# One-hot in spare PSUM columns ahead of the products; nodes' gating and residual tile by tile (a graph network layer on one core)

## The chip, the cores and the metric

The kernel runs on one core of a Trainium2 chip. The time is device time in microseconds (us), the median of three runs. The core has five engines that work at once, each through its own queue in order: PE (matmuls), DVE (elementwise), ACT (activations and copies), POOL (here it issues the indirect loads) and SP (it issues plain loads and stores). SBUF is the working memory, PSUM the small memory that PE writes into. The profile is one execution recorded by the hardware profiler.

## The reference

A layer of message passing on 12,500 nodes with 160 features (64 scalars and 32 vectors of 3) and 400,000 edges, which come sorted by destination. Cut to what matters:

```python
h_s = s @ lin1_ws * a * inv(64);  h_v = einsum('nci,cd->ndi', v, lin1_wv) * a * inv(32)
w   = silu(edge_scalars @ fc_w1 * inv(64)) @ fc_w2 * inv(64)      # 224 weights per edge
es, ev = h_s[edge_src], h_v[edge_src]                             # gather, 160 numbers per edge
m_s1 = w1 * es * e0;              m_s2 = w4 * (ev . e1) * inv(3)
m_v1 = (w2 * es) x e1;  m_v2 = w3 * ev * e0;  m_v3 = w5 * cross(ev, e1) * inv(2)
agg  = segment_sum([m_s1, m_s2], [m_v1, m_v2, m_v3], edge_dst) / 4
pre  = self_connection(x) + lin2(agg)
scalars = silu(pre_s[:, :64]);  gates = sigmoid(pre_s[:, 64:96]); gated = gates * pre_v
out  = layernorm(x + concat(scalars, gated))
```

## The kernel before

A first stage of 62 us multiplies all nodes by lin1 and writes the table `h_tab` to DRAM. Then the edges go by in 3125 tiles of 128 edges, four tiles at a time: a *quad*, 782 of them (the last has one tile). Which quad a tile belongs to is fixed in `steps`; `slot_of` is its place in that order.

The order of the work on PE, DVE, ACT and POOL is written out by hand: the loop at L811 issues one step per quad, and each engine runs its instructions in the order in which they are issued there. For quad n a step issues

- `gather` (L448, L452): four indirect loads on POOL, one per tile, each of 128 rows of `h_tab`, into `hg` (four buffers of a quad each, so the gather of quad n+4 reuses the buffer of quad n);
- `weights` (L457, L465): on PE, the edges' 224 weights of each tile into `pw`, a PSUM tile of 4 x 256 columns, of which columns 224 to 255 of each tile are unused. There are two such tiles, used in turn, so quad n+2 writes where quad n was;
- `products` (L469): on DVE, one multiplication at L475 and three at L483, from `pw` (PSUM) and `hg` (SBUF) into `pr`. Between them come pieces of older work (`add_up`, the nodes' `rest`);
- `select_quad` (L523): on DVE, the one-hot `oh` at L529, which compares the edges' relative destinations `rel` with `iota`, and `sel` at L532, the one-hot times the four edge attributes `eas`. All five are in SBUF;
- the additions `add` (L571) into the nodes' sums `acc`, and one step of the nodes' work, `step_on`;
- `sum_up` of quad n-2 (L766, L539): on PE, `sel` transposed times `pr`, into `pa`;
- `hide` of quad n+2 (L443, L445), and, when due, the turning of finished blocks (L548 to L553), their second linear map (L563, L566) and the self connection (L712).

The framework adds the waits. It takes a `pw` tile as one whole here: the matmuls of quad n+2 wait for the last instruction that reads quad n's tile, and a DVE instruction that writes into the tile waits for the quad's matmuls.

Nodes whose edges are all done are finished in jobs of up to four tiles of 128 nodes (`finish`, L574): 23 jobs of four tiles, one of two, and the last of four, whose last tile is not full. A job runs as one step each for turning every tile (L597, L598), `gates` (ACT, L604), `gated` (DVE, L608 and L609, from `z` and `sg` into `y`), `residual` (DVE, L616, `y` plus the nodes' input `xt`), `moments` (L621, L623), `root` (L627) and `norm` (L631, L633, and the store at L636). `z`, `sg`, `y` and `xt` are in SBUF. The last job runs after the loop, in the tail.

Of the kernel before, what the change touches and what calls it, by code (L numbers as in the profile page):

```python
# [10 lines left out]
F32 = mybir.dt.float32  # L11
# [9 lines left out]
P = 128  # L21
S = 64
V = 32
V3 = 3 * V
# [6 lines left out]
W = 16  # L31
Q = 4
# [3 lines left out]
AHEAD = 3 * CT  # L36
# [4 lines left out]
NWT = 224  # L41
# [12 lines left out]
def gnn_kernel(  # L54
# [21 lines left out]
    nc = tc.nc  # L76
# [58 lines left out]
    slot_of = {}  # L135
# [88 lines left out]
    with tc.tile_pool(name="nodes", bufs=len(starts)) as nodes, tc.tile_pool(  # L224
        name="nodes_ps", bufs=6, space=PSUM
# [83 lines left out]
        for c0, cn, quarters, cq, xa, xz in loaded:  # L309
# [3 lines left out]
            nt = -(-cn // P)  # L313
            first = c0 // P
            full = cn // P
            for t0 in range(0, nt, U):
                ps = nps.tile([P, U, P], F32, name="hp")
                for t in range(t0, min(t0 + U, nt)):
                    n = min(P, cn - t * P)
                    nc.tensor.matmul(ps[:n, t - t0], xa[:, t * P:t * P + n], l1,  # L320
                                     start=True, stop=True)
                k = min(U, full - t0)
# [3 lines left out]
                if t0 + k < nt <= t0 + U:  # L326
                    n = cn - full * P
# [6 lines left out]
            for u in range(-(-cq // P)):  # L334
                n = min(P, cq - u * P)
# [10 lines left out]
            if cn > full * P:  # L346
                n = cn - full * P
# [35 lines left out]
    for to, part, pieces, w, r0, c0, by in maps:  # L383
        for k, piece in enumerate(pieces):
# [3 lines left out]
            m = terms.setdefault((to, part, four), len(terms))  # L388
# [131 lines left out]
            sorted_eat[a0] = eas  # L520
        return sorted_eat[a0]

    def select_quad(pool, tiles):  # L523

        n = len(tiles)
        t0 = slot_of[tiles[0][0]]
        u = t0 % AHEAD
        oh = pool.tile([P, Q, W], F32, name="oh4")[:, :n]
        nc.vector.tensor_tensor(oh, rel[:, t0:t0 + n, None].to_broadcast([P, n, W]),  # L529
                                iota[:, None, :].to_broadcast([P, n, W]), op=OP.is_equal)  # L530
        sel = pool.tile([P, Q, 4, W], F32, name="sel", bufs=3)
        nc.vector.tensor_mul(  # L532
            sel[:, :n], oh[:, :, None, :].to_broadcast([P, n, 4, W]),
            by_slot(tiles[0][0])[:, u:u + n, :, None].to_broadcast([P, n, 4, W]))
        return sel
# [38 lines left out]
    def finish(fin, psum, t0, nt, p, most=NF):  # L574


        whole = nt if p == P else nt - 1
        xt = fin.tile([P, most, D], F32, name="xt", bufs=2)
        held = []
        if whole < nt:  # L580
            nc.vector.memset(xt[:, whole], 0.0)
        parts = [(slice(t0 * P, (t0 + whole) * P), slice(0, whole), P)] if whole else []
        if whole < nt:
            parts.append((slice((t0 + whole) * P, (t0 + whole) * P + p), slice(whole, nt), p))
        for nodes_of, k, n in parts:
            nc.sync.dma_start(xt[:n, k], x[nodes_of, :].rearrange("(t p) d -> p t d", p=n))

        def turn(k):
            if not held:
                held.extend(fin.tile([P, most, *shape], F32, name=name) for name, shape in (  # L590
                    ("z", [2 * V3]), ("sg", [V3]), ("y", [D]), ("st", [6]), ("mv", [2]),
                    ("rs", [])))
            z = held[0]
            c = (t0 + k) * P
            pp = psum.tile([P, 2, V3], F32, name="pp", tag="misc")
            for m in range(2):
                nc.tensor.transpose(pp[:, m], acc[:, m, c:c + P], ident[:V3, :V3])  # L597
            return lambda: nc.vector.tensor_scalar(  # L598
                z[:, k], pp.rearrange("p m c -> p (m c)"), at[:, t0 + k:t0 + k + 1], None,
                op0=OP.mult)  # L600

        def gates():
            z, sg = held[:2]
            nc.scalar.activation(sg[:, :nt], z[:, :nt, :V3], AF.Sigmoid)  # L604

        def gated():
            z, sg, y = held[:3]
            nc.vector.tensor_mul(y[:, :nt, :S], z[:, :nt, :S], sg[:, :nt, :S])  # L608
            nc.vector.tensor_mul(  # L609
                y[:, :nt, S:].rearrange("p t (c i) -> p t i c", i=3),  # L610
                z[:, :nt, V3:].rearrange("p t (i c) -> p t i c", i=3),
                sg[:, :nt, None, S:].to_broadcast([P, nt, 3, V]))

        def residual():
            y = held[2]
            nc.vector.tensor_add(y[:, :nt], y[:, :nt], xt[:, :nt])  # L616

        def moments():
            _, _, y, st, mv, _ = held
            for k in range(nt):  # L620
                nc.vector.bn_stats(st[:, k], y[:, k])  # L621
            for k in range(nt):
                nc.vector.bn_aggr(mv[:, k], st[:, k])  # L623

        def root():
            mv, rs = held[4:]
            nc.scalar.activation(rs[:, :nt], mv[:, :nt, 1], AF.Sqrt, bias=eps)  # L627

        def norm():
            _, _, y, _, mv, rs = held  # L630
            nc.vector.reciprocal(rs[:, :nt], rs[:, :nt])  # L631
            for k in range(nt):
                nc.vector.tensor_scalar(y[:, k], y[:, k], mv[:, k, 0:1], rs[:, k:k + 1],  # L633
                                        op0=OP.subtract, op1=OP.mult)
            for nodes_of, k, n in parts:
                nc.sync.dma_start(out[nodes_of, :].rearrange("(t p) d -> p t d", p=n), y[:n, k])  # L636

        return [lambda k=k: turn(k) for k in range(nt)] + [
            gates, gated, residual, moments, root, norm]


    tiles_of_nodes = -(-N // P)
# [5 lines left out]
    with tc.tile_pool(  # L648
        name="fin", bufs=1
# [132 lines left out]
        def add_up(n):  # L782

            if not adds or adds[0][0] > n:
                return []
            _, b, os, k, base = adds.pop(0)
            waiting.discard(blocks_of(b // 2)[b % 2])
            return [(base, os, k)]
# [15 lines left out]
        with tc.manual_schedule(engines={ENG.PE, ENG.DVE, ENG.Activation, ENG.Pool}):  # L804
            fetch(0)
            hide(0)
            waits = []
            pieces = list(range(0, N, CHN))
            products_due = []
            checks = farthest(late)  # L810
            for n, (c, i, tiles) in enumerate(steps):  # L811
                if 2 <= n < 2 + ZP // 2:
                    for k in range(2):
                        clear(2 * (n - 2) + k)
                if n in checks:
                    checks[n]()
                fetch(n + 4)
                hg = gather(deep, [index(t) for t, _, _ in tiles])
                pw = weights(pw_ps, hids[c, i // 2], [(half, u - i // 2 * 4) for _, half, u in tiles])

                rest = turning.pop(0)() if turning else None
                step_on = not rest and doing.pop(0) if doing and not turning and not rest else None
                ready = []

                def first(n=n):
                    if rest:
                        rest()
                    ready.extend(add_up(n))

                pr = products(edge, pw, hg, len(tiles), [first, lambda n=n: ready.extend(add_up(n))])  # L830
                sel = select_quad(edge, tiles)
                for a in ready:
                    add(*a)
                if step_on:
                    step_on()
                begin()
                waits.append((tiles, pr, sel))
                if len(waits) > 2:
                    sum_up(n, *waits.pop(0))
                hide(n + 2)  # L840
                for blocks, in due(maps_due, n):
                    output(n, blocks)
                for j, sa in due(turns_due, n):
                    turn_blocks(n, j, sa)
                if products_due:
                    products_due.pop(0)()()
                if n % 30 == 13 and pieces:
                    products_due.extend([lambda: (lambda: None)] * 3 + self_connection(pieces.pop(0)))
            assert not pieces and not products_due
            last_steps = finish(fin, misc_ps, *last_job, most=LAST)  # L850
            n = len(steps)
            while waits:
                sum_up(n, *waits.pop(0))
            while turns_due or maps_due:
                n += 1
                for blocks, in due(maps_due, n):
                    output(n, blocks)
                for j, sa in due(turns_due, n):
                    turn_blocks(n, j, sa)
            assert len(adds) <= NO  # L860
            n += 2
            while adds:
                for a in add_up(n) + add_up(n):
                    add(*a)
            while turning or doing or to_do:
                begin()
                for f in turning:
                    f()()
                for f in doing:
                    f()  # L870
                turning.clear()
                doing.clear()
            for f in last_steps[:LAST]:
                f()()
            for f in last_steps[LAST:]:
                f()
# [113 lines left out]
```

## Time and profile before

| | |
|---|---|
| median of three runs | 4050.34 us (4040.81, 4050.34, 4052.72) |
| the profiled execution: its time, its span | 4037.76 us, 4036.0 us |
| granted TensorE clock, mean | 0.965 |
| first gather starts, last gather ends | 61.74 us, 4003.11 us |
| busy, first stage (0 to 62 us) | PE 37.64, DVE 29.36, ACT 3.46, POOL 14.52 us |
| busy, one stretch of the loop (2000 to 3000 us) | PE 916.83, DVE 605.60, ACT 230.25, POOL 758.95 us |
| busy, tail (4003 to 4036 us) | PE 16.70, DVE 14.43, ACT 8.94, POOL 0.11 us |

An engine's busy time counts its instructions, not what its queue spends between them. A row of the groups of instructions reads: line, engine, operation, output<-inputs with their shapes, count | busy us, mean ns of one | idle us of that engine just before them, and who ended most of it. The loop is even: its three stretches of a thousand microseconds (1000 to 4003) differ by less than 1% in the busy time of PE, DVE and POOL.

### The profile page before, as it was taken

To read this page: it belongs to the slowest core of one execution; us is meant where nothing else is said; L and a number is where in the kernel's file an instruction comes from. 1 tells how busy PE (TensorE), PEld (TensorE's weight loads), DVE (VectorE), ACT (ScalarE), POOL (GpSimd) and SP (SyncE) were. 2 spreads that over 40 slices of the span, in tenths; PEclk is the share of its full clock that TensorE was granted. 3 is DMA by queue.
4 is the path that set the end of the run, shared out by engine and by line. 5 is a ranking of instruction groups with operands and counts; after the bars stand their busy time and mean duration, and the time that the engine had idled before them with its cause. 6 is when DMAs were issued, how large, how long until landed. Compare 5 with 4: busy or idle time off the path is not lost. (4 is left out here: it accounts for less than half of the span.)

```text
span 4036.0 us, 46681 instructions
## 1 busy us (share of the span) xinstructions
PE 3679.1 (91%) x14291; PEld 1590.5 (39%) x14291; DVE 2436.6 (60%) x6386; ACT 939.4 (23%) x2463; POOL 3003.9 (74%) x3144
## 2 busy tenths in 40 slices
PE   6999899999989999989998999899898999999997
PEld 4344343333334433333333334334343333333443
DVE  5656655665655655656656656556665665655665
ACT  2222121221222222212212222122122221222222
POOL 4777777777777777777777777777777777777775
PEclk8999999999999999999999999999999999999999
DMA  8344443444444434444444444444444443444442
GB/s 242 94 99 96 98 105 94 104 103 94 104 96 100 107 93 101 105 96 101 106 94 100 95 104 102 94 105 98 98 105 95 105 101 94 103 101 97 98 97 57
DMA packets 227691, 411.71 MB, mean 102 GB/s; under 512 B 71883, under 2 KB 157383, under 8 KB 226535
## 3 DMA queue, kind: packets, MB, share of 16 engines
q0 software_dynamic: 152272, 266.53, 27.6%
q1 hardware_dynamic: 74646, 142.01, 14.7%
q8 instruction: 115, 1.88, 0.2%
q14 instruction: 144, 1.18, 0.1%
q10 hardware_dynamic: 514, 0.10, 0.0%
HBM read 392.41 MB, written 16.00 MB: 101 GB/s over the span
## 5 line engine op out<-in xcount | busy, mean ns | idle before, releaser
L452 POOL DMA_INDIRECT hg<-h_tab,idx x3125 | 2989.7, 957 | 958.5 <-issue 866.6
L465 PE MATMUL pw<-w,hid 128*128 128x448 f32 x3126 | 1376.1, 564 | 194.4 <-DVE pr L483 165.7
L475 DVE TENSOR_TENSOR pr<-pw,hg 128x512 f32<-128x512 f32 x782 | 539.8, 690 | 1460.8 <-DMA hg<-h_tab,idx 967.6
L539 PE MATMUL pa<-pr,sel 128*64 128x416 f32 x6250 | 1307.9, 540 | 0.0
L483 DVE TENSOR_TENSOR pr<-pw,hg 128x384 f32<-128x384 f32 x2346 | 1153.8, 547 | 0.0
L465 PEld LDWEIGHTS pw<-w,hid 128*128 128x128 f32 x3126 | 555.6, 194 | 680.7 <-issue 442.2
L539 PEld LDWEIGHTS pa<-pr,sel 128*64 128x64 f32 x6250 | 389.6, 140 | 820.2 <-issue 680.8
L732 ACT COPY sa<-pa 128x416 f32<-128x416 f32 x521 | 263.7, 506 | 1450.4 <-PE pa L539 1447.9
L443 PE MATMUL misc<-es,w 128*128 128x512 f32 (+1 forms) x784 | 449.4, 656 | 15.6 <-DMA es<-in_es_t_dram 13.8
L445 ACT ACTIVATE hid<-misc 128x512 f32<-128x512 f32 x392 | 233.6, 596 | 739.3 <-PE misc L443 738.8
L548 PEld LDWEIGHTS misc<-ident,sa 128*128 128x128 f32 x2084 | 240.0, 141 | 310.3 <-issue 250.9
L532 DVE TENSOR_TENSOR sel<-oh,eas 128x256 f32<-128x256 f32 x782 | 338.3, 433 | 38.6 <-DVE oh L529 0.9
L563 PE MATMUL misc<-tt,l 128*96 128x256 f32 (+5 forms) x1496 | 346.1, 379 | 3.5 <-DVE z L598 2.0
L548 PE MATMUL misc<-ident,sa 128*128 128x128 f32 x2084 | 327.5, 280 | 0.8 <-DVE acc L713 0.7
L551 ACT COPY tt<-misc 128x192 f32<-128x192 f32 x521 | 164.8, 316 | 513.1 <-PE misc L548 510.6
L563 PEld LDWEIGHTS misc<-tt,l 128*96 128x96 f32 (+1 forms) x1496 | 227.0, 162 | 141.6 <-issue 73.0
L443 PEld LDWEIGHTS misc<-es,w 128*128 128x128 f32 x784 | 119.3, 192 | 283.1 <-issue 228.2
L571 DVE TENSOR_TENSOR acc<-acc,os 96x32 f32 x1042 | 193.5, 186 | 25.9 <-ACT os L566 6.9
L529 DVE TENSOR_TENSOR oh<-rel,iota 128x64 f32<-128x64 int16 x782 | 170.5, 218 | 0.0
L597 PE MATMUL misc<-ident,acc 96*128 96x96 f32 x196 | 36.8, 274 | 103.8 <-DVE acc L571 83.6
L553 ACT COPY tt<-misc 128x64 f32<-128x64 f32 x521 | 116.6, 224 | 0.0
L566 ACT COPY os<-misc 96x512 f32<-96x512 f32 (+2 forms) x68 | 38.3, 564 | 303.3 <-PE misc L563 282.7
(84 smaller groups left out, 633.3 us busy)
## 6 DMA issues: line engine op xcount, KB each, us to landing
es<-in_es_t_dram SPq DMA_DIRECT2D x258, 384.0 KB
hg<-h_tab,idx POOLq DMA_INDIRECT x3125
h_tab<-ht POOLq DMA_DIRECT2D x6, 1280.0 KB
xt<-in_x_dram SPq DMA_DIRECT2D x23, 320.0 KB
out_dram<-y SPq DMA_DIRECT2D x23, 320.0 KB
xv<-in_xv_t_dram SPq DMA_DIRECT2D x25, 187.5 KB
xs<-in_xs_t_dram SPq DMA_DIRECT2D x25, 125.0 KB
xa<-in_xs_t_dram SPq DMA_DIRECT2D x6, 512.0 KB
```

The costliest lines, as they stand in the source:

```text
L443: nc.tensor.matmul(ph[:k, c], w1[:k, :k], es[:k, t0 * P + c0 * P:t0 * P + c1 * P], start=True, stop=True)
L445: nc.scalar.activation(hid[:k, c], ph[:k, c], AF.Silu, scale=1.0 / math.sqrt(64))
L452: nc.gpsimd.indirect_dma_start(out=hg[:, t, :], out_offset=None, in_=h_tab, in_offset=bass.IndirectOffsetOnAxis(ap=i, axis=0))
L465: nc.tensor.matmul(pw[:, t:t + m, :NWT], hid[:m * S, c * P:(c + 1) * P], w2[:m * S, :m], start=True, stop=True)
L475: nc.vector.tensor_mul(two, pw[:, :n, :2 * S].rearrange("p t (k c) -> p t k c", k=2), hg[:, :n, None, :S].to_broadcast([P, n, 2, S]))
L483: nc.vector.tensor_mul(pr[:, :n, first:first + V3].rearrange("p t (i c) -> p t i c", i=3), pw[:, :n, None, 2 * S + k * V:2 * S + (k + 1) * ...
L532: nc.vector.tensor_mul(sel[:, :n], oh[:, :, None, :].to_broadcast([P, n, 4, W]), by_slot(tiles[0][0])[:, u:u + n, :, None].to_broadcast([P ...
L539: nc.tensor.matmul(pa[half * ROWS:(half + 1) * ROWS, :NPR], sel[:, t].rearrange("p k w -> p (k w)"), pr, start=start, stop=stop)
L548: nc.tensor.transpose(pt[:, four * P:four * P + k], sa[:k, c:c + P], ident[:k, :k])
L563: nc.tensor.matmul(po[:, k, :nb], l2[r, terms[to, part, four]], a[:, :nb], start=(n == 0), stop=(n == len(of) - 1))
L571: nc.vector.tensor_add(window, window, os[:, :, b])
L732: nc.scalar.copy(sa, pas.pop(j)[:, :NPR])
```

## The change

The one-hot moves from a buffer in SBUF into columns 224 to 239 of each tile of the quad's `pw`, and its instruction moves ahead of the four products; the selection reads it there and stays behind the products. In `finish`, all jobs but the last do the gating and the residual with one instruction per tile of 128 nodes in place of one for all tiles of the job.

```diff
-    def select_quad(pool, tiles):
+    def one_hot(tiles, pw):
 
         n = len(tiles)
         t0 = slot_of[tiles[0][0]]
-        u = t0 % AHEAD
-        oh = pool.tile([P, Q, W], F32, name="oh4")[:, :n]
+        oh = pw[:, :n, NWT:NWT + W]
         nc.vector.tensor_tensor(oh, rel[:, t0:t0 + n, None].to_broadcast([P, n, W]),
                                 iota[:, None, :].to_broadcast([P, n, W]), op=OP.is_equal)
+        return oh
+
+    def select_quad(pool, tiles, oh):
+
+        n = len(tiles)
+        u = slot_of[tiles[0][0]] % AHEAD
         sel = pool.tile([P, Q, 4, W], F32, name="sel", bufs=3)
         nc.vector.tensor_mul(
             sel[:, :n], oh[:, :, None, :].to_broadcast([P, n, 4, W]),
...
         whole = nt if p == P else nt - 1
+        spans = [(0, nt)] if t0 + nt == tiles_of_nodes else [(k, k + 1) for k in range(nt)]
...
         def gated():
             z, sg, y = held[:3]
-            nc.vector.tensor_mul(y[:, :nt, :S], z[:, :nt, :S], sg[:, :nt, :S])
-            nc.vector.tensor_mul(
-                y[:, :nt, S:].rearrange("p t (c i) -> p t i c", i=3),
-                z[:, :nt, V3:].rearrange("p t (i c) -> p t i c", i=3),
-                sg[:, :nt, None, S:].to_broadcast([P, nt, 3, V]))
+            for k, m in spans:
+                nc.vector.tensor_mul(y[:, k:m, :S], z[:, k:m, :S], sg[:, k:m, :S])
+                nc.vector.tensor_mul(
+                    y[:, k:m, S:].rearrange("p t (c i) -> p t i c", i=3),
+                    z[:, k:m, V3:].rearrange("p t (i c) -> p t i c", i=3),
+                    sg[:, k:m, None, S:].to_broadcast([P, m - k, 3, V]))
 
         def residual():
             y = held[2]
-            nc.vector.tensor_add(y[:, :nt], y[:, :nt], xt[:, :nt])
+            for k, m in spans:
+                nc.vector.tensor_add(y[:, k:m], y[:, k:m], xt[:, k:m])
...
+                oh = one_hot(tiles, pw)
                 pr = products(edge, pw, hg, len(tiles), [first, lambda n=n: ready.extend(add_up(n))])
-                sel = select_quad(edge, tiles)
+                sel = select_quad(edge, tiles, oh)
```

## The prediction

> **What bounds the kernel now.** I read the page's busy shares first, then its groups of instructions (busy us, mean ns | idle us before them and who ended it):
>
> ```profile
> PE 3679.1 (91%) x14291; PEld 1590.5 (39%) x14291; DVE 2436.6 (60%) x6386; ACT 939.4 (23%) x2463; POOL 3003.9 (74%) x3144
> ...
> L452 POOL DMA_INDIRECT hg<-h_tab,idx x3125 | 2989.7, 957 | 958.5 <-issue 866.6
> L465 PE MATMUL pw<-w,hid 128*128 128x448 f32 x3126 | 1376.1, 564 | 194.4 <-DVE pr L483 165.7
> ...
> L483 DVE TENSOR_TENSOR pr<-pw,hg 128x384 f32<-128x384 f32 x2346 | 1153.8, 547 | 0.0
> ...
> L532 DVE TENSOR_TENSOR sel<-oh,eas 128x256 f32<-128x256 f32 x782 | 338.3, 433 | 38.6 <-DVE oh L529 0.9
> ...
> L529 DVE TENSOR_TENSOR oh<-rel,iota 128x64 f32<-128x64 int16 x782 | 170.5, 218 | 0.0
> ```
>
> PE's 91% draws the eye, but the gathers on POOL (L452) decide. Their 2989.7 us busy and 958.5 us before them make 3948.2 us. The first starts at 61.74 us, after 6.87 us of that idle time, so the row fills the span from 54.87 to 4003.1 us without a hole. The view of the line's own instructions gives min/median/max:
>
> ```profile
> L452 POOL DMA_INDIRECT hg<-h_tab,idx x3125: 942/946/1670, 61.7 to 4002.2; - x196
> ```
>
> Over the trace's gathers I counted the pause before each next one: 303 to 313 ns, always, so POOL never waits for a buffer, PE or DVE. 2903 of 3125 gathers last 942 to 955 ns, 945.6 on average. The span is therefore 61.7 us of start + 3125 x (946 + 305 ns) = 3909 us + what single gathers last longer + 33 us behind the last one. That third term is 2989.7 - 3125 x 0.946 = 33.4 us, and it is all that this change can win on POOL. The timeline shows what makes it (start, us, engine, line):
>
> ```profile
> 712.23 0.42 DVE L608 TENSOR_TENSOR y<-z,sg 128x256 f32<-128x256 f32 x1
> 712.38 1.61 POOL L452 DMA_INDIRECT hg<-h_tab,idx  x1 [0.30 <-DMA hg<-h_tab,idx]
> ...
> 712.57 0.67 DVE L609 TENSOR_TENSOR y<-z,sg 128x384 f32<-128x384 f32 x1
> ...
> 716.77 0.81 DVE L616 TENSOR_TENSOR y<-y,xt 128x640 f32<-128x640 f32 x1
> 716.80 1.61 POOL L452 DMA_INDIRECT hg<-h_tab,idx  x1 [0.30 <-issue]
> ...
> 1181.67 0.42 DVE L532 TENSOR_TENSOR sel<-oh,eas 128x256 f32<-128x256 f32 x1
> 1181.72 1.20 POOL L452 DMA_INDIRECT hg<-h_tab,idx  x1 [0.30 <-issue]
> ...
> 2001.90 1.48 DVE L483 TENSOR_TENSOR pr<-pw,hg 128x384 f32<-128x384 f32 x3
> ...
> 2002.19 0.95 POOL L452 DMA_INDIRECT hg<-h_tab,idx  x1 [0.30 <-issue]
> ```
>
> The selection of 1181.67 ends at 2.09, and the gather that began at 1.72 lasts 1.20 us, not 0.95. The residual of 716.77 costs its gather 0.66 us; the gating pair of 712.23 and 712.57 costs 0.66 us, held through both. Three products (2001.90) lie over a gather that keeps its 0.95. The difference: selection, gating and residual have both inputs in SBUF, a product reads pw from PSUM. Laid against all gathers, the rule of the rows is sharp. A DVE instruction with two SBUF inputs that starts at least 40 ns before the gather and ends over 127 ns after the gather's start (192 for L609) lengthens it by exactly the excess; one that starts later costs it almost nothing. By the instruction whose end fits, the 33.4 us are: sel L532 151 gathers, 23.5 us; L616 9, 4.4; L609 12, 4.0; L608 3, 0.4; oh L529 25, 1.2; others, at the start above all, about 1, less rounding. Products: 3128 instructions, one gather, 0.02 us.
>
> A check on size: with starts spread evenly over a period of 1251 ns, an instruction of length d costs (d - 167)²/(2 x 1251) ns. For sel (425 ns at the median) that is 26.6 ns x 782 = 20.8 us (23.5 counted), for oh (216) 0.8 us (1.2 counted), for the three node instructions 298 ns x 24 = 7.2 us (8.8 counted).
>
> **The change part by part.** (1) *sel reads its one-hot from PSUM.* It then has the products' form, one input in PSUM and one in SBUF. Bounds: 23.5 us won (the product rows) to 0 (if the SBUF input alone were what blocks; the 2346 L483 rows, with one SBUF input each, speak against it). I take 23.5. Its own length: the product rows give 690 ns for 512 and 547 for 384, so 0.40 us for 256 against 0.43 now; nothing changes.
>
> The Trainium skill, "SBUF — State Buffer", section "Who interferes with whom", has a sentence that speaks against all this: a two-input tensor_tensor was seen not to stall DMAs, since descriptor generation needs the write interface and it takes only the read one (marked there as inferred). By that sentence part 1 would be worth 0; the rows of 716.80 and 1181.72 above say that here it does stall, so the rows stand.
>
> (2) *oh is written to PSUM, ahead of the products.* rel and iota stay in SBUF, so it keeps blocking. No row shows DVE writing PSUM; the nearest are 164 ns (16 elements) and 218 (64) into SBUF and 291 (a 128-element product out of PSUM), and I take 218. What can change is its place in the gather's period, now the end of pw's matmuls or of DVE's work before it: computed from the old trace, 20 to 37 of 782 such points fall into the 50 ns that block, at shifts of up to 150 ns. I take 1.2 us as now, 0 net; bounds +1.2 (never) and 782 x 51 ns = 40 lost (always at the worst point). On DVE it is a 0.22 us move, plus about 0.04 us of gap between oh and its reader, which now falls before the products. In 61% of quads DVE idles at least 0.26 us there (page: 1460.8 us in all), which hides it; elsewhere the products end 0.26 us later and sel no later than now.
>
> (3) *The wait that moves.* A pw bank pair is now free for quad n+2's matmuls when sel n has read it, not when the third product has: 0.43 + 0.04 us later. Queued on PE behind L465 are the sums L539 of quad n, which need that sel anyway. Today the wait shows as
>
> ```profile
> PE pw L465 <- DVE pr L483: 165.7, 78, 5.5
> ```
>
> so 78 of 782 quads feel it; 78 x 0.47 = 37 us more PE idle. What is late next is products n+2, then the freeing of hg, then the gather of quad n+6. From the third product of n to the first gather of n+4 the trace has 10.9 us at the median, 7.6 at the 5th percentile, 3.4 at least after the first five quads (0.6 at 82.7 us, once). 0.5 us is lost in that: 0, bound 1 us at the start. Uncovered, it is the third rival.
>
> (4) *Gating and residual tile by tile* in 23 jobs of four tiles and one of two (the last job is unchanged): 2 + 1 instructions become 8 + 4. The rows by shape:
>
> ```profile
> L616 DVE TENSOR_TENSOR y<-y,xt 128x640 f32<-128x640 f32 x24 | 19.6, 817 | 0.0
> ...
> L609 DVE TENSOR_TENSOR y<-z,sg 128x384 f32<-128x384 f32 x24 | 16.3, 678 | 0.0
> L608 DVE TENSOR_TENSOR y<-z,sg 128x256 f32<-128x256 f32 x24 | 10.0, 417 | 0.6 <-ACT sg L604 0.6
> ...
> L616 DVE TENSOR_TENSOR y<-y,xt 128x320 f32<-128x320 f32 x1 | 0.5, 479 | 0.0
> ...
> L609 DVE TENSOR_TENSOR y<-z,sg 128x192 f32<-128x192 f32 x1 | 0.4, 406 | 0.0
> ...
> L608 DVE TENSOR_TENSOR y<-z,sg 128x128 f32<-128x128 f32 x1 | 0.3, 282 | 0.0
> ```
>
> The last three are the two-tile job, so each length has two points: fixed 141 to 147 ns (L609 135) plus 1.056 ns per element (L609 1.41). One tile costs 214 (L608), 271 (L609), 310 ns (L616); a job 4 x 795 = 3.18 us against 1.91, so 23 x 1.27 + 0.4 = 30 us more on DVE, inside its 1599 us of idle time, since no gather or sum of that step waits for y. For the gathers the formula gives 4 x (0.9 + 4.3 + 8.2) = 53 ns a job, 1.3 us in all. But 1 of the 4 gathers that L608 held was held on through L609 without a gap. With a quarter held on, 0.94 held gathers a job x 1/3 x 0.25 us adds 0.08 us a job, 1.9 in all. So 3.3 us stay of 8.8: 5.5 won. Bounds: 8.8 won, and a loss: were each train of pieces held as one block (1.94 and 1.24 us), 1.7 us a job, 40 us in all, 31 more than now.
>
> (5) No DMA moves: SP's and POOL's queues keep their orders, out's transfer is issued from the same step. In the tail (33 us) the last job keeps its long instructions; the last full quad waits for its gather (1.84 us idle), so oh is hidden there: 0 to 0.3 us won, taken as 0.
>
> Sum: 23.5 + 5.5 = 29.0 us. The profiled execution took 4037.8 us for its span of 4036.0; it becomes 4007.0 and 4008.8. It lies 12.6 us below the median of 4050.3, under all three timed runs. I know no row for that offset, so I take 29.0 from the mean of all four executions, 4045.4: **4016**.
>
> **Rivals.** *A: sel blocks from PSUM as well* and only part 4 works: 4045.4 - 5.5 = 4040. For: half its input still comes from SBUF, and the edit doesn't take oh's own two SBUF inputs away. Against: the L483 rows. *B: the pieces hold like one train:* 4045.4 - 23.5 + 31 = 4053. For: 712.38; against: three of four freed at L608's end. *C, the slower one: the later release of pw makes PE the pace.* PE needs 3679.1/782 = 4.70 us a quad, POOL afterwards 4 x 1.252 = 5.01, so 0.30 us is spare. If all quads felt the 0.47 us, each would cost 0.17 us more, 133 us in all: 4149. It decides from 0.30/0.47, 64% of the quads, on; today 10% wait there, and PE has 357 us of idle time already. Half of this price is still slower by over 1%.
>
> **How the numbers follow.** Forecast 0.82, A 0.07, B 0.04, C 0.05, an unseen gain or loss of a few us around the bound 0.02. A measurement here tells 0.3% (12 us) from no change; 4038 is the border. Forecast and little else falls under it: faster 0.84, same (A, B) 0.10, slower (C) 0.06. Range: below, the floor of POOL 61.7 + 3909 + 33 = 4004, about all 33 us won and no offset; above, half of sel's gain with the offset, 4050.3 - 12 = 4038.
>
> **What would show it.** The gather row near 2961 us (mean 947 or 948, not 957), pause still 305 ns; sel over gathers of 0.95 us; oh with about its 1.2 us; L465's wait now on sel, longer than 165.7 us, without a gap in POOL. I am wrong if gathers of 1.1 to 1.2 us still end with sel, if pauses over 0.31 us appear on POOL (C), or if trains of small gating pieces end gathers of over 1.3 us (B).

## The result and the profile after

The changed kernel takes 4018.96 us, the median of six runs (4017.94 to 4022.50); before takes 4043.76 us over six runs, the three shown and three more. The ratio is 0.9935, 95% interval 0.9922 to 0.9948: 25 us, 0.65%, shorter.

The page of the changed kernel (busy shares, then groups of instructions; lines behind `select_quad` have moved: oh is L528, sel L537, the sums L544):

```profile
PE 3676.3 (92%) x14291; PEld 1588.0 (40%) x14291; DVE 2410.5 (60%) x6596; ACT 938.7 (23%) x2463; POOL 2982.9 (74%) x3144
...
L452 POOL DMA_INDIRECT hg<-h_tab,idx x3125 | 2968.7, 950 | 962.2 <-issue 865.5
L465 PE MATMUL pw<-w,hid 128*128 128x448 f32 x3126 | 1376.5, 564 | 191.5 <-DVE sel L537 150.1
...
L528 DVE TENSOR_TENSOR pw<-rel,iota 128x64 f32<-128x64 int16 x782 | 178.4, 228 | 468.3 <-PE pw L465 465.5
...
L537 DVE TENSOR_TENSOR sel<-pw,eas 128x256 f32<-128x256 f32 x782 | 323.6, 414 | 0.0
```

Gathers last 2968.7 us in all, not 2989.7, and the mean is 950 ns, not 957. The pauses between them are 303 to 315 ns, all 3124, as before: POOL still paces and still waits for nobody. The span fell by 19.0 us, from 4036.0 to 4017.0: 21.0 us shorter gathers, a first gather that starts 3.7 us later (65.42 against 61.74 us) and a tail 1.7 us shorter.

The timeline around one selection (start, us, engine, line):

```profile
2438.48 0.41 DVE L537 TENSOR_TENSOR sel<-pw,eas 128x256 f32<-128x256 f32 x1
...
2438.55 0.95 POOL L452 DMA_INDIRECT hg<-h_tab,idx  x1 [0.30 <-issue]
```

This sel starts 67 ns before the gather and ends 0.35 us after the gather's start. By the prediction's rule that position would have cost 0.22 us; now the gather has its 0.95. Over the whole trace 254 sels stand where they would have held a gather, and these gathers last 945.5 ns on average, none over 960. The next lines are the nodes' residual in four pieces:

```profile
3605.81 1.02 DVE L624 TENSOR_TENSOR y<-y,xt 128x160 f32<-128x160 f32 x4
...
3606.19 1.59 POOL L452 DMA_INDIRECT hg<-h_tab,idx  x1 [0.30 <-issue]
...
3606.75 0.22 DVE L528 TENSOR_TENSOR pw<-rel,iota 128x64 f32<-128x64 int16 x1
```

The gather at 3606.19 is held through the pieces and on through the one-hot that follows them at 3606.75: 1.59 us, as long as the gather under the single long residual (1.61 us at 716.80 before).

The excess of the gathers over 946 ns, by the instruction whose end fits, in us (a count over each trace; "to oh's end" are gathers held by node pieces and let go at the end of a one-hot directly behind; "oh alone" are all others let go at its end, also those that began under an addition or a sel ahead of it. Their sum is firm, the split between these two columns only to about 1 us):

| kernel | gathers in all | sel | nodes | nodes, to oh's end | oh alone |
|---|---|---|---|---|---|
| before | 2989.7 | 23.5 | 8.8 | 0 | 1.2 |
| changed | 2968.7 | 0 | 3.4 | 6.8 | 2.5 |
| e1 one-hot's part alone | 2965.0 | 0 | 3.9 | 2.1 | 2.5 |
| e2 tile by tile alone | 3006.0 | 33.8 | 8.0 | 0 | 1.2 |
| e3 one-hot ahead, in SBUF | 2995.1 | 19.1 | 0.3 | 15.2 | 4.0 |
| e4 one-hot in PSUM, behind | 2967.1 | 0 | 8.7 | 0 | 1.2 |
| e5 iota in PSUM too | 2963.3 | 0 | 8.1 | 0 | 0 |
| e6, e10 one piece a step | 2966.7, 2960.3 | 0 | 3.3, 3.5 | 0 | 0 |

The runs e1 to e4 were on a chip like that of the result, but e5 to e12 were on three chips where the granted TensorE clock was 0.87 to 0.89 on average and not 0.96 and before itself takes 5007 to 5067 us, so their times are compared with before on the same chip alone.

### The profile page after: what moved, and what is told of

Read it like the earlier page. It is cut to its first block, busy times and chain, and to the rows that moved or that the text cites. A ratio compares the mean times of both kernels' runs of the same rounds, so it can differ in the third digit from the quotient of the medians.

```text
span 4017.0 us, 46675 instructions
## 1 busy us (share of the span) xinstructions
PE 3676.3 (92%) x14291; PEld 1588.0 (40%) x14291; DVE 2410.5 (60%) x6596; ACT 938.7 (23%) x2463; POOL 2982.9 (74%) x3144
## 5 line engine op out<-in xcount | busy, mean ns | idle before, releaser
L452 POOL DMA_INDIRECT hg<-h_tab,idx x3125 | 2968.7, 950 | 962.2 <-issue 865.5
L465 PE MATMUL pw<-w,hid 128*128 128x448 f32 x3126 | 1376.5, 564 | 191.5 <-DVE sel L537 150.1
L544 PE MATMUL pa<-pr,sel 128*64 128x416 f32 x6250 | 1303.5, 539 | 0.0
L544 PEld LDWEIGHTS pa<-pr,sel 128*64 128x64 f32 x6250 | 388.0, 139 | 812.3 <-issue 799.4
L528 DVE TENSOR_TENSOR pw<-rel,iota 128x64 f32<-128x64 int16 x782 | 178.4, 228 | 468.3 <-PE pw L465 465.5
L537 DVE TENSOR_TENSOR sel<-pw,eas 128x256 f32<-128x256 f32 x782 | 323.6, 414 | 0.0
```

The costliest lines, as they stand in the source:

```text
L452: nc.gpsimd.indirect_dma_start(out=hg[:, t, :], out_offset=None, in_=h_tab, in_offset=bass.IndirectOffsetOnAxis(ap=i, axis=0))
L465: nc.tensor.matmul(pw[:, t:t + m, :NWT], hid[:m * S, c * P:(c + 1) * P], w2[:m * S, :m], start=True, stop=True)
L537: nc.vector.tensor_mul(sel[:, :n], oh[:, :, None, :].to_broadcast([P, n, 4, W]), by_slot(tiles[0][0])[:, u:u + n, :, None].to_broadcast([P ...
L544: nc.tensor.matmul(pa[half * ROWS:(half + 1) * ROWS, :NPR], sel[:, t].rearrange("p k w -> p (k w)"), pr, start=start, stop=stop)
```

## The experiments

The theories, by the letters that the expectations use: L, the forecast's, gathers are held by DVE instructions with two SBUF inputs and POOL paces; O, the new order gains; T, the short node pieces gain; W, time on DVE and the wait for pw decide; later R, the time for which pw is occupied.

**e1, the one-hot's part alone.**

```diff
-        spans = [(0, nt)] if t0 + nt == tiles_of_nodes else [(k, k + 1) for k in range(nt)]
+        spans = [(0, nt)]
```

> The one-hot's part alone; gating and residual stay one instruction per job. Theory L (a DVE instruction with two SBUF inputs over a gather's start holds the gather, and POOL paces): sel's 23.5 us are gone as in the changed kernel, the node instructions cost about 9 to 11 us again; the gathers last 2965 to 2972 us in all, time 4015 to 4023, the changed kernel's within 0.1%. Rival T (the short node pieces carry a good part of the gain): at least 5 us longer than the changed kernel, gathers 2974 us or more.

4020.61 us (4014.16 to 4022.87), ratio to before 0.9937 [0.9924, 0.9951]; gathers 2965.0 us. The changed kernel's ratio is 0.9935: as far as the intervals tell (5 us), the whole gain is the one-hot's.

**e2, tile by tile alone:** before's `select_quad`, the changed `finish`.

> Gating and residual tile by tile alone; the one-hot stays in SBUF behind the products. L: sel keeps its 20 to 25 us; trains of pieces hold gathers as the single long instructions did, but behind them come products and not a one-hot, so 5 to 9 us for the nodes; gathers 2985 to 2992 us in all, time 4038 to 4046, no change from before within 0.2%. Rival T: gathers 2983 us or less, time under 4036.

4046.20 us, ratio 1.0004 [0.9995, 1.0013] over 11 runs: no gain, so rival T falls twice. The profiled execution was the longest of the 11 (4056.16 us), and its gathers, 3006.0 us, lie outside what was expected: in it sel held 197 gathers and not 151, 10 us more, and undisturbed gathers took about 2 ns more, 6 us in all. So where sel happens to fall can move an execution by 10 us.

**e3, the changed order, the one-hot in SBUF.**

```diff
-        oh = pw[:, :n, NWT:NWT + W]
+        oh = pool.tile([P, Q, W], F32, name="oh4")[:, :n]
```

> The changed kernel with the one-hot in an SBUF buffer again, but still ahead of the products: the order is the changed one, only the memory differs. L: sel has two SBUF inputs again and costs 18 to 28 us: gathers 2987 to 2997 us, time 4038 to 4050, as slow as before. Rival O (taking the one-hot off the chain behind the gather's landing is what helped): time within 5 us of the changed kernel's 4019.

4046.11 us, ratio 1.0004 [0.9995, 1.0014]. The page of e3:

```profile
L452 POOL DMA_INDIRECT hg<-h_tab,idx x3125 | 2995.1, 958 | 960.3 <-issue 860.6
...
L537 DVE TENSOR_TENSOR sel<-oh,eas 128x256 f32<-128x256 f32 x782 | 324.8, 415 | 0.0
```

sel has the changed kernel's place and length (415 ns against 414) and only the one-hot's memory differs, yet the gathers last 2995.1 us and the gain is gone. Rival O falls; L stands. The node pieces show what they do when sel, adds, pieces and one-hot all have two SBUF inputs and follow one another: 15.2 us held to a one-hot's end.

**e4, the one-hot in PSUM but behind the products.**

```diff
-                oh = one_hot(tiles, pw)
                 pr = products(edge, pw, hg, len(tiles), [first, lambda n=n: ready.extend(add_up(n))])
+                oh = one_hot(tiles, pw)
```

> The changed kernel with the one-hot in PSUM but issued behind the products, ahead of sel. L: sel costs nothing, the one-hot alone 1 to 3 us, and trains of node pieces are no longer followed by the one-hot but by products with a PSUM input, so the 6.8 us of gathers held to the one-hot's end shrink: gathers 2962 to 2967 us in all, time 4011 to 4018, somewhat shorter than the changed kernel. pw is freed 0.23 us later than in the changed kernel; if that wait mattered (rival W), time over 4022 with pauses over 0.32 us on POOL. Rival O: time back near 4040.

4018.56 us (4015.97 to 4024.83), ratio 0.9941 [0.9928, 0.9955], gathers 2967.1 us: the changed kernel's time, not the somewhat shorter one expected. No gather is held to a one-hot's end any more, but the pieces hold 8.7 us among themselves, against 10.1 with the one-hot behind them. The one-hot lasts 236 ns there, longer than in the changed kernel, and yet holds only 1.2 us. Pauses on POOL stay at 312 ns or less: the later release of pw costs nothing here (W falls).

**e5, iota in PSUM too.**

```diff
+            for t in pw_ps.tiles:
+                nc.vector.tensor_copy(t[:, NWT + W:256], iota)
...
-                                iota[:, None, :].to_broadcast([P, n, W]), op=OP.is_equal)
+                                pw[:, 0:1, NWT + W:].to_broadcast([P, n, W]), op=OP.is_equal)
```

> The changed kernel, and iota read from the last 16 spare columns of the same PSUM tile, so that the one-hot too has one SBUF input. L: the one-hot's own 2.5 us go, and trains of node pieces end with their last piece and not with the one-hot: 10.1 us for the nodes become 5 to 8; gathers 2959 to 2965 us, time 4008 to 4015. Rival W (time on DVE and the wait for pw matter, not inputs): no change from 4019.

On a chip with clock 0.88: 5095.52 us, ratio 1.0177 [1.0137, 1.0218]. The gathers are as L expected, 2963.3 us, and no gather is held by a one-hot; the time says nothing on L, since POOL doesn't pace there (e9).

**e6, one node piece a step**, on top of e5: `finish` returns each tile's L615, L616 and L624 as a step of its own for jobs with t0 < 80.

> As the run with iota in PSUM, and for the first 20 jobs only one piece of gating or residual per step, so that a piece stands alone among products with a PSUM input; the later jobs whole, so that the tail is kept. L: 20 jobs at 53 ns a job by the formula are 1 us, the four other jobs 0.37 us each, 1.5 us: nodes 2 to 4 us in all, gathers 2956 to 2960 us, time 4005 to 4012, the shortest of all kernels here. Rival (short pieces alone hold as much as trains): like the run with iota in PSUM.

5108.26 us, ratio 1.0190 [1.0157, 1.0222]. Nodes hold 3.3 us, as expected; the gathers are 2966.7 us, outside it, since in this execution even undisturbed ones took about 2 ns more.

**e7 and e8, the price by itself:** behind each sel one more multiplication of its size, with both inputs in SBUF (e7) or one in PSUM (e8).

```diff
+        spare = pool.tile([P, Q, 4, W], F32, name="spare")
+        nc.vector.tensor_mul(spare[:, :n], X.to_broadcast([P, n, 4, W]),
+                             by_slot(tiles[0][0])[:, u:u + n, :, None].to_broadcast([P, n, 4, W]))
```

X is `iota[:, None, None, :]` in e7 and `oh[:, :, None, :]` in e8.

> The changed kernel and, behind each selection, one more multiplication of the same size with both inputs in SBUF (iota by the edge attributes) whose result nobody reads. L: (425 - 167)^2/(2 x 1251) ns x 782 = 21 us by the formula, up to 30 where node pieces and adds follow and lengthen the train: gathers 2988 to 3000 us, time 4039 to 4052. Rival W: equal to the same kernel with a PSUM input.

> The same extra multiplication with one input in PSUM (the one-hot) and one in SBUF, so the same DVE time, 0.41 us x 782 = 324 us more, and pw freed 0.41 us later still. L: costs nothing on POOL: gathers 2966 to 2972 us, time 4016 to 4024. Rival W: 20 us or more above the changed kernel.

5119.65 us, ratio 1.0222 [1.0179, 1.0264], and 5132.77 us, ratio 1.0243 [1.0192, 1.0294], on one chip with clock 0.88. The page of e7, then that of e8:

```profile
L452 POOL DMA_INDIRECT hg<-h_tab,idx x3125 | 2992.7, 958 | 1974.2 <-DVE pr L483 1035.6
...
L541 DVE TENSOR_TENSOR spare<-iota,eas 128x256 f32<-128x256 f32 x782 | 344.1, 440 | 0.0
```

```profile
L452 POOL DMA_INDIRECT hg<-h_tab,idx x3125 | 2966.3, 949 | 2064.6 <-DVE pr L483 1101.4
...
L541 DVE TENSOR_TENSOR spare<-pw,eas 128x256 f32<-128x256 f32 x782 | 324.4, 415 | 0.0
```

782 instructions more on each, 440 and 415 ns long. In e7 111 of them stand where they would hold a gather, and 108 of these gathers last over 960 ns, 1080 on average; in e8 105 stand there, and no such gather lasts over 955 ns, 945 on average. The gathers let go at the end of e7's extra instruction make 15.1 us, where the formula gave 21 and the expectation 21 to 30. The rows differ by more, 2992.7 - 2966.3 = 26.4 us, but 9 us of that are undisturbed gathers, which took 948 ns in e7's execution and 945 in e8's, so that e7's total lies in its range partly by luck. The hold is shown by itself; that it becomes time, as e3 showed, can't be seen on this chip.

**e9 and e10, the changed kernel and e6 again**, side by side.

> The changed kernel itself, as the yardstick beside the next run on the same chip. The last four runs were on a chip whose TensorE clock was granted at 0.88 instead of 0.96, where before took 5020 us, POOL waited for DVE's products (gaps of up to 11 us) and all four variants were 1.8 to 2.4% slower than before. Theory L with POOL as the pace: where before takes about 4044, this takes 4015 to 4023 (ratio 0.993 to 0.995). Where before is near 5000 (PE as the pace), rival C of the prediction (a pw pair freed 0.47 us later): 1 to 2.5% slower than before; if L alone held there, no slower than before.

> The kernel with iota in PSUM and one piece of the nodes' gating or residual per step, again. Its gathers were 2966.7 us long with 3.3 us of it held by node pieces, none by the one-hot or sel; on an undisturbed chip the 13 us of small rests should go. L: gathers 2956 to 2962 us, time 8 to 13 us under the changed kernel on the same chip where before takes about 4044 (4006 to 4013). Rival: within 3 us of the changed kernel. Where before is near 5000: the same as the changed kernel within 1%, since gathers don't pace there.

Again clock 0.87 to 0.88. The changed kernel: 5087.13 us, ratio 1.0157 [1.0122, 1.0193], *slower* than before by 80 us. e10: 5107.68 us, ratio 1.0213 [1.0184, 1.0242], though its gathers are the shortest of all, 2960.3 against 2965.6 us. The page of e9, and the clock of the changed kernel's page behind it (tenths of full speed in 40 slices):

```profile
PE 4003.2 (78%) x14291; PEld 1713.1 (34%) x14291; DVE 2445.4 (48%) x6596; ACT 925.1 (18%) x2463; POOL 2979.9 (58%) x3144
...
PEclk8888898898988889889898888888888888988888
...
L452 POOL DMA_INDIRECT hg<-h_tab,idx x3125 | 2965.6, 949 | 2034.3 <-DVE pr L483 1080.5
```

```profile
PEclk8999999999999999999999999999999999999999
```

POOL's idle time before its gathers is 2034.3 us, 962.2 in the result's trace, and products end over half of it: here POOL waits for buffers, and the length of the gathers doesn't show in the time (e7's are 26 us longer than e8's, its median 13 us shorter). The timeline of e9 shows PE standing:

```profile
1143.64 0.60 PE L553 MATMUL misc<-ident,sa 128*128 128x128 f32 x4
...
1153.19 1.98 PE L720 MATMUL misc<-xv,scv 96*96 96x500 f32 x2 [8.95 <-issue]
```

No matmul of the trace starts between 1144.24 and 1153.19 us, 8.95 us for which the profile shows no wait ("issue"). Behind the first gather 130 gaps of over 3 us make 793 us in e9, and 41 make 167 us in the result's trace; only 35 of the 130 name "issue", and what stops PE stays open. The lower clock goes with these gaps (the trace shows full or half clock): 162 of the 175 stretches at half clock in e9, and 47 of the 48 in the result's trace, begin in or within 4 us behind a gap of over 1.5 us, at the median 3.2 and 3.5 us after the gap's start. So a mean clock of 0.88 is first of all a sign that PE stands more often; that the clock itself makes these chips slow is not shown.

**e11 and e12, the release of pw.** e11 is e6 with sel too ahead of the products; e12 is e3 again.

> The kernel with iota in PSUM and one piece of the nodes' work per step, and the selection too ahead of the products, directly behind the one-hot (it needs nothing of the gather). Where before takes about 4044 and POOL paces: no gather is held by sel or the one-hot, nodes 3 to 4 us, gathers 2956 to 2962 us, time 4005 to 4013, the shortest here. Where before takes about 5000 and POOL waits: what counts by theory R (the time from the end of pw's matmuls to the last reader of pw, which frees it for the quad after next) is the sum of the DVE work on pw, which the order doesn't change: 1.6 to 2.4% slower than before, like the two runs with sel behind. If sel's place at the end were what costs: 1% slower or less.

> The changed kernel with the one-hot in SBUF, ahead of the products, again. Where before takes about 4044: equal to before within 0.2% as in the first run of it. Where before takes about 5000: by R pw is freed behind the third product, 0.27 us later than before (the one-hot ahead) and not 0.68 (one-hot and sel); at the 80 us per 0.68 us that the changed kernel lost there, 20 to 40 us, 0.4 to 0.8% slower than before. If the one-hot's place ahead of the products alone is the cause: 1.2% or more. If PSUM as the one-hot's place is: no slower than before.

Clock 0.88. e11: 5183.04 us, ratio 1.0236 [1.0199, 1.0272]; sel's place at the end isn't what costs. Its gathers, 2964.7 us, lie outside what was expected: lone pieces held 79 of them, 9.4 us, where sel no longer stands between the products and the pieces. Of the 79, 50 began behind a pause of over 330 ns, none in e6 or e10: POOL had waited, and started where the pieces stand. e12: 5089.04 us, ratio 1.0034 [1.0005, 1.0064], 17 us by the ratio and 22 between the medians, at the low edge of the 20 to 40 expected. So with the one-hot ahead in SBUF a fifth of e9's loss (on another chip) is there, and most comes when sel reads pw: it then occupies pw for 0.41 us more. PE's waits for the release of pw (us, times, longest) fit that, in e12 and then in e9:

```profile
PE pw L465 <- DVE pr L483: 47.4, 30, 8.5
```

```profile
PE pw L465 <- DVE sel L537: 102.1, 47, 5.8
```

That is 55 us more in e9, where the losses differ by about 60. It agrees with R, but R is not shown. e8 occupies pw about 0.41 us longer than e7 on the same chip, 48 us by the rate of 80 us per 0.68 us, and is 13 us slower, within the two intervals (PE's waits for the release: 100.4 and 87.3 us). And e9, e10 and e11 have the same DVE work on pw and lie between 1.0157 and 1.0236.

## Why the prediction was right, and where not

- *POOL paces, PE doesn't.* Right: pauses of 303 to 315 ns before and after, up to 324 in e1 to e4.
- *Part 1, sel:* 23.5 us forecast, 23.5 us gone; e3 brings 19.1 of them back by the memory alone, e7 against e8 shows the same hold on another instruction, 15.1 us against none. How many sels meet a gather is chance (151, in e2 197), so that the size came out exactly is partly luck. The sentence of the Trainium skill's "SBUF — State Buffer", "Who interferes with whom", by which a two-input tensor_tensor doesn't stall DMAs, doesn't hold for these gathers: in e7 it stalls 108. The forecast named that sentence alone, but the same section also says that a DVE instruction with two SBUF inputs contends with a GpSimd instruction that reads SBUF, and these gathers take their row numbers `idx` from SBUF; that this reading is what is held, no run here shows.
- *Part 2, oh:* 0 net forecast; 1.3 us lost (2.5 against 1.2). It lasts 228 ns in PSUM, not 218, but that isn't the reason: in e4 it lasts 236 ns and holds 1.2 us. Its new place is: ahead of the products it follows additions and sel directly, and a hold that begins under an addition passes to it (seven gathers, 0.7 us, in the result's trace). The forecast had looked at its place in the gather's period alone.
- *Part 3, the wait for pw:* 37 us more idle time on PE were forecast, hidden. It was hidden, and the releaser changed as said, but the wait didn't grow:

```profile
PE pw L465 <- DVE sel L537: 150.1, 89, 5.3
```

  150.1 us over 89 waits against 165.7 over 78, so the term of 78 x 0.47 us was wrong. From the last product of a quad to the gather that reuses its buffer there were never less than 4.8 us. Hidden it is where POOL paces; in e9 the cover is gone.
- *Part 4, the pieces:* the failed step. 5.5 us won were forecast; 10.1 us are held instead of 8.8, so 1.3 us were lost (a difference that chance could make; the 5.5 are missing in e2 too, where 8.0 us are held). The rows by shape and the timeline show why:

```profile
L616 DVE TENSOR_TENSOR y<-z,sg 128x96 f32<-128x96 f32 x94 | 26.5, 282 | 0.0
...
L624 DVE TENSOR_TENSOR y<-y,xt 128x160 f32<-128x160 f32 x94 | 24.1, 316 | 0.0
...
L615 DVE TENSOR_TENSOR y<-z,sg 128x64 f32<-128x64 f32 x94 | 20.2, 215 | 0.0
```

  The lengths are as worked out (271, 310 and 214 ns). But the timeline starts each piece before the last one ends (four residuals of 0.316 us fill 1.02 us), and I let a hold pass from one to the next one time in four, from four long pairs. Counted in the result's trace, a hold passed 55 of 66 such borders; to a product it passed at none of 27 (e2 and e4). Once caught, a gather is mostly kept to the end of the train, and the one-hot at its end lengthens it. That is rival B's mechanism, and B's sign is there, gathers of over 1.3 us at the end of trains. B's price, 40 us, isn't: the trains last 1.30 and 1.02 us, not 1.94 and 1.24, which by the formula makes 19 us, and a hold that passes only most borders makes less. Of 43 gathers that start inside a train, where they could be held, 37 are, 10.0 us in all; held to the train's end they would lose 18.1. Pieces that stand alone hold less, 3.3 us in e6 against 8.1 in e5 on the same chip.
- *The sum:* 29.0 us forecast, 21.0 in the gathers, which the parts explain: 23.5 - 1.3 - 1.3 = 20.9. Between the medians it is 25; the other four are not explained. The profiled execution of before, 4037.76 us, was shorter than all six timed ones, and of those there is no trace. The start, which the sum left unchanged, scatters: the first gather begins at 61.7, 65.4, 68.2, 62.8, 63.6 and 63.1 us in before, the result and e1 to e4. The mean of four executions as the base, 4045.4, was near before's median of six, 4043.8; so with the sizes found the forecast would have been 4045.4 - 20.9 = 4024.5. That 4016 came within 3 us of 4019 is in part luck: 8 us too much in the sum, against a base 1.6 us too high and the four unexplained ones.
- *Rival C* was given 0.05, and on the chip of e9 its outcome is there, 80 us slower. I had worked out that it decides when PE loses its 0.30 us per quad. In e9 PE's own work takes 4003.2/782 = 5.12 us a quad, more than POOL's 5.01, and its long gaps come on top, so the 0.30 us are gone without any more waits for pw. That the later release of pw is then what costs is argued and not shown (e12 against e9 speaks for it, e8 against e7 for less). Why the loss there is 1.6% for the change and 2.1 to 2.4% for e10 and e11 is open: no trace of before was taken on such a chip.
- *Not shown:* the time of e5, e6 and e11 where POOL paces. On one chip e10's gathers are 5 us shorter than the changed kernel's.

## What to carry to other kernels

Where an engine runs back to back, don't look at what waits for it but at the spread of its own instruction's length: here 7% of the gathers held all that could be won, and laying each against the other engines gave the cause, and its price in that execution. An input moved from SBUF to PSUM can free a neighbour engine even if its own instruction is no faster; splitting a long instruction into pieces that follow each other freed next to nothing here, while pieces that stand alone held less (e6), unless the neighbour's start was tied to them (e11). A gain taken from a buffer's slack, here pw held longer, holds only while the engine that paces stays the same, so compare on a chip where another engine paces too.

## What the runs showed of the hardware

- A DVE instruction with two SBUF inputs that starts at least some 40 ns before a gather lengthens it by what it lasts beyond the gather's first 127 ns. With one input in PSUM, 868 products (before) and 254 sels (result) stood like that, and one of these gathers lasted over 960 ns.
- A hold passes from one such instruction to the next when they overlap, 55 of 66 times for short pieces, the longest gather of the result's trace lasting 2035 ns; to a product, none of 27 times.
- A one-hot written to PSUM takes 228 ns (236 behind the products, e4), to SBUF 218 (216 in e3); sel from PSUM 414, from SBUF 433 behind its one-hot and 415 apart from it (e3).
- The same kernel takes 4044 us on one chip and 5007 to 5067 on three others, with a mean granted TensorE clock of 0.96 and 0.88. In e9, on one of the three, PE starts nothing in 130 gaps of over 3 us, the longest 14.6 us (41 in the result's trace), and nearly all stretches at half clock begin in or just behind a gap.
